# Differential attention of the last batch in pieces among the experts, and the order of the row chains' leads

## The chip, the cores and the metric

The kernel runs on one core of a Trainium2 chip, in fp32 throughout. The metric is device time in microseconds (us), the median of several runs. Engines: TensorE (PE; its weight loads are listed as PEld), VectorE (DVE), ScalarE (ACT), GpSimd (POOL) and SyncE (SP, which here only issues DMAs). A scatter or gather by index and an adding DMA are issued by POOL, all plain loads and stores by SP.

## The reference, cut to what matters

`x` has 8 batches of 512 positions of 128 numbers. There are two layers; in each, an attention and a feed-forward part read the same normalised `x`, and both are added to it. The change touches layer 1 alone.

```python
xn = layernorm(x)                            # layer 0 has been added to x
x  = x + diff_attn(xn) + ffn(xn)

def diff_attn(x):                            # for each batch, 512 x 512
    a = softmax(q1 @ k1.T * s) - lam * softmax(q2 @ k2.T * s)
    o = a @ v
    return o / sqrt(mean(o * o) + EPS) * 0.2

def ffn(h):                                  # "rows": along the 8 batches, for each position
    qkv = layernorm(h) @ Wqkv                # 16 query heads, 8 key/value heads
    h   = h + causal_attention(qkv) @ Wproj  # 8 x 8 scores for each position and head
    z   = layernorm(h)
    p   = softmax(z @ Wrouter)               # 8 experts, the best 2 of each token
    put z of each token into the slots of its two experts (1280 slots for each expert)
    for e in experts:                        # 128 -> 512 -> 128
        y = gelu(slots[e] @ W1[e]) @ W2[e] * weight
        add the rows of y to the rows of h they came from
    return h
```

The output is thus written in parts: `x` with the differential attention and `h` first, then the rows of the experts are added to it in DRAM.

## The kernel before, in words

**Stages on the trace.** Layer 0's feed-forward part and the projections run to about 278 us. A long loop over layer 0's attention follows to about 706; beside it run the first *row chains* of layer 1. A row chain is a generator for batch `s_` (its code begins above L690): normalise, project to `qkv`, eight products of the batch's query with all earlier keys on POOL (L722), each summed into a score buffer `sc` on DVE (L714 to L717), softmax, products with the values on POOL (L751) and their sums `l_at` on DVE (L760), a transpose `a1T_p` and a projection `pp` on TensorE (L782), the second normalisation, the router on POOL and TensorE (L812 to L889), and eight indirect DMAs (*puts*, L896) that write the batch's rows into the experts' slots `xs`. Chain 7 is the last. `sc` has one buffer, and L703 holds a chain until the chain before it has passed that point.

**Leads.** The chains in flight are `leads`. `step_leads` (L1162) is called once for each step of the main work and lets each lead do one piece, if the kind that it has named (`"pe"`, `"pool"`, `"dve"`, `"act"`) has room in this step; one POOL piece in all, given to the oldest lead that wants it.

**The tail** (L1374 to L1382) comes after the loop, from about 714 to 906 us. Its main work is the generator `diff(range(8))` (L1327): for each batch four projections `pqk` (L1246), a value `pv` (L1254), two scores `s` for each of four tiles of 128 queries (L1270) with a maximum on DVE (L1274) and an Exp on ACT (L1275), the combination of both on DVE (L1288), a transpose `dT`, an output `po` (L1304) and its squares on ACT (L1308). After the fourth tile POOL makes the reciprocal root `ri` (L1313 to L1316, four instructions), `diff_end` adds `po * ri` to `x_all` on DVE (L1321), and `store` sends the batch's 256 KB to the output by SP (L1369). The rows' chains 5, 6 and 7 are fed by `step_leads` at each step. The scores use the buffers "d" of PSUM, the projections and transposes the two buffers "t", the outputs "o".

`in_order(tail)` (L1382) then ties every instruction of the tail on PE, DVE, ACT and POOL to the one emitted before it on the same engine. So in the tail the order of emission is the order of execution. What is emitted after it, the experts, may be arranged by a scheduler.

**The experts** (L1391 to L1448), to the end: for each of eight experts a load `xe` of 1280 slots by SP (L1393, which waits for all puts), the slots' weights and row numbers on DVE (`first`, `wt`, `to`), and three blocks of 4, 4 and 2 tiles: a transpose with a copy `xeT` on DVE (L1413), up matmuls `phm` (L1421) with Gelu on ACT (L1424), down matmuls `pem` (L1428), a scaling `es` on DVE (L1434), and for each tile an indirect DMA on POOL (*scatter*, L1439) that adds 128 rows to the output. Scatters of one expert may overlap; those of the next one wait until all rows of the one before have landed, and expert 0's until all eight stores have.

```python
for name in backs[e] if e else bases:                                # L1446
    tc.add_manual_dep(back.ins, name, sync, ...)
```

Of the kernel before, what the change touches and what calls it, by code (L numbers as in the profile page):

```python
# [9 lines left out]
F32 = mybir.dt.float32  # L10
# [8 lines left out]
P = 128  # L19
# [6 lines left out]
def kernel(ctx: ExitStack, tc: tile.TileContext, a: dict, out: bass.AP):  # L26
# [579 lines left out]
    lw = {}  # L606
# [28 lines left out]
    def ln_stats(name, rows):  # L635
        stt = small.tile([P, 4, 6], F32, tag="bn_st", name=f"st_{name}")
        mv = small.tile([P, 4, 2], F32, tag="bn_mv", name=f"mv_{name}")
        for k, r in enumerate(rows):
            dve.bn_stats(out=stt[:, k, :], in_=r)
            dve.bn_aggr(out=mv[:, k, :], in_=stt[:, k, :])  # L640
            yield 1, "dve"
        yield 1, "pool"
        rs = small.tile([P, 4], F32, tag="bn_rs", name=f"rs_{name}")
        rsqrt(rs, mv[:, :, 1])
        nmr = small.tile([P, 4], F32, tag="nmr", name=f"nmr_{name}")
        nc.gpsimd.tensor_scalar(out=nmr, in0=mv[:, :, 0], scalar1=-1.0, scalar2=None, op0=ALU.mult)
        nc.gpsimd.tensor_tensor(out=nmr, in0=nmr, in1=rs, op=ALU.mult)
        yield 5, ""
        return mv, rs, nmr
# [15 lines left out]
    def lead(s_):  # L665
# [36 lines left out]
        yield 3, "pool"  # L702
        yield from after("sc", s_ - 1)  # L703
        sc = wt("sc", [NI * H, NB])
        q = qkv[:, s_, :, :, 0:2].rearrange("p i v r s -> p (i v) r s")
# [14 lines left out]
        for t in range(n):  # L720
            pr = prod("q", t)
            nc.gpsimd.tensor_tensor(out=pr, in0=of(t, 2), in1=q, op=ALU.mult)  # L722
            behind.append((t, pr))
            if len(behind) > BEHIND:
                yield 1, "dve"
                sum_q(*behind.pop(0))
            if t + 1 < n:
                yield 1, "pool"
# [20 lines left out]
        for t in range(n):  # L749
# [8 lines left out]
            if len(behind) > BEHIND:  # L758
                yield 1, "dve"
                dve.tensor_tensor(out=at4, in0=at4, in1=behind.pop(0), op=ALU.add)  # L760
# [129 lines left out]
        passed.add(("route", s_))  # L890
        yield 3, "pool"

        for i in range(NI):
            m = s_ * NI + i
            for k in range(2):
# [7 lines left out]
                puts.append(put.ins.name)  # L903
                yield 1, "pool"
        passed.add(("z2", s_))
# [3 lines left out]
    with ExitStack() as at:  # L909
# [251 lines left out]

        def step_leads(slot_, pe_free, pool_free, more):  # L1162
            room[0] = min(room[0] + more, more)
            spare[0] = min(spare[0] + more * SPARE, CAPA * more)
            for r in list(leads):
                if slot_ < r[1] or (r[2] == "pe" and not pe_free) or (r[2] == "pool" and not pool_free):
                    continue
                if r[2] == "dve" and room[0] <= 0 or r[2] == "act" and spare[0] <= 0:
                    continue
                if r[2] == "pool":  # L1170
                    pool_free = False
                nxt = next(r[0], None)
                if nxt is None:
                    leads.remove(r)
                else:
                    r[1], r[2] = slot_ + nxt[0], nxt[1]
# [49 lines left out]
    with ExitStack() as l1b:  # L1226
# [8 lines left out]
        cols = l1p["cols"]  # L1235
        wka = l1b.enter_context(tc.tile_pool(name="wka", bufs=2, reuse_waits="tile"))


        ascale = D ** (-0.25)
        OUT = (1.0 - LAMBDA_INIT) * math.sqrt(D)  # L1240
        dd = {}

        def diff_qk(b):
# [16 lines left out]
        def diff_scores(b, i):  # L1260
# [7 lines left out]
            for k in range(2):  # L1268
                sc = psum_t(f"s1_{u}_{k}", "d")
                nc.tensor.matmul(  # L1270
# [27 lines left out]
        def diff_out(b, i):  # L1298
            if i == 0:
                dd["po", b] = psum_o(f"po1_{b}")  # L1300
                dd["ss", b] = small.tile([P, NI], F32, tag="ss1", name=f"ss1_{b}")
            po, dT, ss = dd["po", b][:, i * D : (i + 1) * D], dd["dT", b, i], dd["ss", b]
            for c in range(NI):
                nc.tensor.matmul(  # L1304
                    po, lhsT=dT[:, c * P : (c + 1) * P], rhs=dd["v", b][:, c], start=(c == 0), stop=(c == NI - 1),
                )
            junk = wka.tile([P, D], F32, tag="sqj1", name=f"sqj1_{b}_{i}")
            nc.scalar.activation(junk, po, AF.Square, scale=1.0 / OUT, accum_out=ss[:, i : i + 1])  # L1308
# [9 lines left out]
        def diff_end(b):  # L1318
            po, ri = dd["po", b], dd["ri", b]
            for i in range(NI):  # L1320
                nc.vector.scalar_tensor_tensor(  # L1321
                    out=x_all[:, b, i], in0=po[:, i * D : (i + 1) * D], scalar=ri[:, i : i + 1],
                    in1=x_all[:, b, i], op0=ALU.mult, op1=ALU.add,
                )
            store(b)

        def diff(bs):  # L1327
# [8 lines left out]
            yield from diff_scores(*us[2])  # L1336
            more = diff_qk(bs[1])
            for m, (b, i) in enumerate(us):
# [29 lines left out]
        def store(b):  # L1368
            bases.append(  # L1369
                nc.sync.dma_start(out=out[b].rearrange("(i p) d -> p i d", p=P), in_=x_all[:, b]).ins.name  # L1370
            )

        slot_ = 4 * (N3 + 4)
        tail = len(nc.cur_bb.bb.instructions)  # L1374
        run = diff(range(NB))
        going = True
        while going or leads:
            going = next(run, "end") != "end"
            for _ in range(1):
                step_leads(slot_, True, True, 9.0)  # L1380
                slot_ += 1
        in_order(tail)  # L1382
        l1.close()
# [6 lines left out]
        backs = [[]]  # L1390
        for e in range(NE):  # L1391
            xe = wk.tile([P, NCT, W], F32, tag="xe", name=f"xe_{e}", bufs=3)
            get = nc.sync.dma_start(out=xe, in_=xs[e * CAP : (e + 1) * CAP].rearrange("(c p) d -> p c d", p=P))  # L1393
            for name in puts:
                tc.add_manual_dep(get.ins, name, sync, reason="any token may be in this expert's slots")

            first = small.tile([P, NCT], F32, tag="first", name=f"first_{e}", bufs=2)
            nc.vector.tensor_scalar(
# [6 lines left out]
            nc.vector.tensor_scalar(out=to, in0=xe[:, :, D + 2], scalar1=FAR, scalar2=None, op0=ALU.add)  # L1405
            es = wk.tile([P, NCT, D], F32, tag="es", name=f"es_{e}", bufs=4)
            backs.append([])
            for c0 in range(0, NCT, 4):
                n = min(4, NCT - c0)
                w = n * P  # L1410
                t = transpose4(f"xeT_p{e}_{c0}", [xe[:, c0 + k, :D] for k in range(n)])
                xeT = wk.tile([P, T], F32, tag="xeT", name=f"xeT_{e}_{c0}")
                nc.vector.tensor_scalar(  # L1413
                    out=xeT[:, :w], in0=t[:, :w], scalar1=cols[:, 2:3], scalar2=cols[:, 3:4], op0=ALU.mult, op1=ALU.add
                )
                hT = wk.tile([P, NHC, T], F32, tag="hTm", name=f"hTm_{e}_{c0}")
                for hp in range(NHC // 2):
                    ph = psum_s(f"phm_{e}_{c0}_{hp}")
                    for k in range(2):
                        hc = 2 * hp + k  # L1420
                        nc.tensor.matmul(  # L1421
                            ph[:, k, :w], lhsT=w1_1[:, e, hc * P : (hc + 1) * P], rhs=xeT[:, :w], start=True, stop=True
                        )
                    nc.scalar.activation(hT[:, 2 * hp : 2 * hp + 2, :w], ph[:, :, :w], AF.Gelu)  # L1424
                pe = psum_o(f"pem_{e}_{c0}")
                for k in range(n):
                    for hc in range(NHC):
                        nc.tensor.matmul(  # L1428
                            pe[:, k * D : (k + 1) * D], lhsT=hT[:, hc, k * P : (k + 1) * P], rhs=w2_1[:, e, hc, :],
                            start=(hc == 0), stop=(hc == NHC - 1),  # L1430
                        )
                for k in range(n):
                    c = c0 + k
                    nc.vector.tensor_scalar(  # L1434
                        out=es[:, c], in0=pe[:, k * D : (k + 1) * D], scalar1=wt_[:, c : c + 1], scalar2=None,
                        op0=ALU.mult,
                    )

                    back = nc.gpsimd.indirect_dma_start(  # L1439
                        out=out_rows, out_offset=bass.IndirectOffsetOnAxis(ap=to[:, c : c + 1], axis=0),  # L1440
                        in_=es[:, c], in_offset=None, bounds_check=NB * T - 1, oob_is_err=False,
                        compute_op=ALU.add,
                    )
                    tc.declare_no_dep(back.ins, group=f"backs{e}", reason="an expert's rows differ")
                    tc.add_to_no_dep_group(f"backs{e}", back.ins)
                    for name in backs[e] if e else bases:  # L1446
                        tc.add_manual_dep(back.ins, name, sync, reason="a row is read and written by each addition")
                    backs[e + 1].append(back.ins.name)  # L1448

# [36 lines left out]
```

## Time and profile before

| | us |
|---|---|
| median of the runs (3) | 1086.97 |
| lowest and highest run | 1086.4, 1087.47 |
| the profiled execution | 1084.87 |
| its span (first to last instruction) | 1083.1 |
| busy PE, PEld, DVE, ACT, POOL from 975 to 1035 us (one stretch of experts) | 58.4, 43.6, 15.2, 15.9, 45.2 of 60 |
| granted TensorE clock, mean of the span | 0.949 |

How to read it: the profile is one execution. A row of a timeline gives the start, the length, the engine, the line, the operation with output and input, and in brackets how long the engine had stood idle before it and what released it; "issue" means that nothing seen held it. "x8" is eight instructions in a row. An fp32 matmul shows as two records of TensorE, and the clock that the chip granted stands beside the work, as a share of full speed. The span ends with the landing of the last scatter. Landing times from issue, by the page's list: the slots' load 4.7 us, a store 2.2, a scatter 3.2, a put 2.3.

```profile
xe<-xs SPq DMA_DIRECT2D x8, 660.0 KB, 4.7
...
out_dram<-x_all SPq DMA_DIRECT2D x8, 256.0 KB, 2.2
out_dram<-es,to POOLq DMA_INDIRECT x80, 3.2
xs<-l_z,sput POOLq DMA_INDIRECT x64, 2.3
```

### The profile page before, as it was taken

The page shows a single profiled execution, that of the slowest core. Times are in us where ns is not written, and L with a number is a line of the kernel's source. Part 1 is how long each engine was busy: PE and PEld are TensorE (multiplying, and loading weights), DVE is VectorE, ACT ScalarE, POOL GpSimd, SP SyncE. Part 2 cuts the span into 40 slices and gives each one's busy share as a digit, 9 for nine tenths or more (in the row PEclk, how much of TensorE's full clock was granted, in tenths as well). Part 3 has the DMA queues.
Part 4 walks back from the last instruction along what each step waited for, and adds up shares of the span by engine and source line. Part 5 has one row for each costly group of instructions (what it writes and reads, how often), then busy time and mean ns, then how long its engine had stood idle before and what let it go on. Part 6 is the DMA issues. An engine that isn't in the chain of part 4 may idle for free.

```text
span 1083.1 us, 18816 instructions
## 1 busy us (share of the span) xinstructions
PE 974.5 (90%) x6726; PEld 599.0 (55%) x6726; DVE 664.2 (61%) x2126; ACT 553.0 (51%) x1263; POOL 565.6 (52%) x793
## 2 busy tenths in 40 slices
PE   6889899989999999999899999978867987999992
PEld 3457556867545454454444444435545655777772
DVE  6734643277777788888778887258676654222220
ACT  3466348353467576766565656527454653222220
POOL 3201000201242527775878879775867361777776
PEclk8999999999799999999999999779988998999997
DMA  8730000000000000000000000050000013342312
GB/s 252 158 85 2 1 1 1 2 2 1 1 1 2 2 1 2 21 2 2 14 9 3 19 2 21 2 172 1 20 11 20 21 38 103 49 67 38 31 15 25
DMA packets 49310, 32.97 MB, mean 30 GB/s; under 512 B 12232, under 2 KB 44275, under 8 KB 49216
## 3 DMA queue, kind: packets, MB, share of 16 engines
q1 hardware_dynamic: 34832, 24.80, 8.6%
q0 software_dynamic: 13568, 6.70, 4.5%
q8 instruction: 53, 0.87, 0.3%
q14 instruction: 41, 0.34, 0.1%
q10 hardware_dynamic: 816, 0.26, 0.1%
HBM read 17.56 MB, written 17.07 MB: 32 GB/s over the span
## 4 chain that ended last, share of the span: by engine, by line
PE 64%; POOL 14%; DVE 11%; issue 5%; ACT 2%; DMA 2%; POOLq 0%; DVEq 0%; SPq 0%; ACTq 0%
PE se L1068 12%; PE pem L1428 7%; PE phm L1421 6%; PE po L1093 6%; POOL xs L896 4%; PE sm L1035 3%; PE lg_d L302 3%; PE pe L477 3%; PE psl L346 3%; DVE junk L1045 2%; PE pf L379 2%; PE pq L955 2%; PE lg_c L302 2%; PE ph L451 2%; PE s L1270 2%
## 5 line engine op out<-in xcount | busy, mean ns | idle before, releaser
L1045 DVE CUSTOM_DVE_ANT_0 junk<-sm,cmask 128x128 f32<-128x128 f32 (+3 forms) x512 | 249.5, 487 | 69.3 <-PE sm L1035 31.2
L1073 ACT ACTIVATE pt<-se 128x384 f32<-128x384 f32 (+1 forms) x384 | 185.4, 527 | 158.7 <-PE sm L1035 109.7
L1035 PE MATMUL sm<-kj,qT 32*128 32x256 f32 (+3 forms) x1024 | 231.6, 487 | 5.7 <-DVE mcol L1045 3.0
L1068 PE MATMUL se<-q,kj 32*128 32x128 f32 (+3 forms) x1024 | 211.3, 483 | 3.9 <-DVE mcol L1045 3.5
L1439 POOL DMA_INDIRECT out_dram<-es,to x80 | 124.0, 1551 | 46.8 <-issue 22.8
L1068 PEld LDWEIGHTS se<-q,kj 32*128 32x128 f32 x1024 | 99.3, 190 | 84.7 <-DVE mcol L1045 26.1
L1078 POOL TENSOR_SCALAR_AFFINE_SELECT pt<-pt 128x512 f32<-128x512 f32 (+1 forms) x96 | 80.1, 835 | 115.8 <-ACT pt L1073 115.6
L1035 PEld LDWEIGHTS sm<-kj,qT 32*128 32x128 f32 x1024 | 112.6, 191 | 23.8 <-DVE mcol L1045 10.1
L1093 PE MATMUL po<-pt,vpad 128*18 128x512 f32 (+3 forms) x1024 | 91.4, 454 | 12.6 <-POOL pt L1078 12.6
L1424 ACT ACTIVATE hTm<-phm 128x1024 f32<-128x1024 f32 (+1 forms) x48 | 42.2, 881 | 109.2 <-PE phm L1421 109.2
L1428 PEld LDWEIGHTS pem<-w,hTm 128*128 128x128 f32 x640 | 77.1, 192 | 16.8 <-ACT hTm L1424 12.1
L1428 PE MATMUL pem<-w,hTm 128*128 128x128 f32 x640 | 81.2, 278 | 0.5 <-ACT hTm L1424 0.2
L1275 ACT ACTIVATE ex<-s,nm 128x512 f32<-128x512 f32 x64 | 43.9, 687 | 70.3 <-DVE nm L1274 69.7
L1434 DVE TENSOR_SCALAR es<-pem,wt 128x128 f32<-128x128 f32 x80 | 22.9, 345 | 90.0 <-PE pem L1428 90.0
L1421 PE MATMUL phm<-xeT,w 128*128 128x512 f32 (+1 forms) x192 | 75.2, 523 | 2.3 <-DVE xeT L1413 2.3
L896 POOL DMA_INDIRECT xs<-l_z,sput x64 | 65.8, 1028 | 17.0 <-issue 16.0
L508 POOL TENSOR_TENSOR x_all<-x_all,bo_bc 128x512 f32<-128x512 f32 x8 | 10.2, 1275 | 119.4 <-DVE xn L266 119.4
L1270 PE MATMUL s<-qk,qk 128*128 128x512 f32 x128 | 63.9, 620 | 6.6 <-ACT qk L1248 6.4
L1093 PEld LDWEIGHTS po<-pt,vpad 128*18 128x18 f32 x1024 | 20.9, 98 | 64.1 <-POOL pt L1078 24.0
L1274 DVE TENSOR_REDUCE nm<-s 128x1 f32<-128x512 f32 x64 | 42.9, 682 | 9.0 <-PE s L1270 8.6
L1421 PEld LDWEIGHTS phm<-xeT,w 128*128 128x128 f32 x192 | 33.6, 191 | 23.1 <-issue 17.2
L722 POOL TENSOR_TENSOR l_prod<-l_qkv 128x512 f32<-128x512 f32 x36 | 45.6, 1277 | 0.6 <-DVE l_at L616 0.6
(262 smaller groups left out, 1865.4 us busy)
## 6 DMA issues: line engine op xcount, KB each, us to landing
xs<-cmask SPq DMA_DIRECT2D x1, 5280.0 KB, 23.8
xe<-xs SPq DMA_DIRECT2D x8, 660.0 KB, 4.7
x_all<-in_L_attn_x_dram SPq DMA_DIRECT2D x8, 256.0 KB, 4.6
w<-in_L_ffn_w_dram SPq DMA_DIRECT2D x1, 2048.0 KB, 8.8
w<-in_L_ffn_moe_w_dram SPq DMA_DIRECT2D x1, 2048.0 KB, 10.0
out_dram<-x_all SPq DMA_DIRECT2D x8, 256.0 KB, 2.2
out_dram<-es,to POOLq DMA_INDIRECT x80, 3.2
xs<-l_z,sput POOLq DMA_INDIRECT x64, 2.3
```

What stands on the lines that cost most here:

```text
L302: nc.tensor.matmul(lg, lhsT=lhs(k), rhs=rhs, start=True, stop=True)
L896: put = nc.gpsimd.indirect_dma_start(out=xs, out_offset=bass.IndirectOffsetOnAxis(ap=sput[:, k, m : m + 1], axis=0), in_=z2[:, i], in_offs ...
L1035: nc.tensor.matmul(sc[:, o : o + w], lhsT=st["qT", b][rr, i * P : (i + 1) * P], rhs=st["k", b, j][rr, :w], start=True, stop=True,)
L1045: nc.vector.tensor_tensor_reduce(out=junk[:, :w], in0=sc[:, o : o + w], in1=cmask[:, 512 - w : 512], scale=-1.0, scalar=BIG, op0=ALU.add, ...
L1068: nc.tensor.matmul(sc[:, o : o + w], lhsT=st["k", b, j][rr, c * P : (c + 1) * P], rhs=st["q2", b, (g % G) // 2][rr, c * P : T], start=True ...
L1073: nc.scalar.activation(st["pt", g, k][:, r, :o], sc[:, :o], AF.Exp)
L1078: nc.gpsimd.affine_select(out=pt[:, :, :n, :P], in_=pt[:, :, :n, :P], pattern=[[0, 4], [0, n], [1, P]], compare_op=ALU.is_ge, fill=0.0, ba ...
L1093: nc.tensor.matmul(po[32 * r : 32 * r + 2 * PW, c * P : T], lhsT=vpads[b % 3][:, c, at_ : at_ + 2 * PW], rhs=pt[:, r, o : o + w], start=(c ...
L1270: nc.tensor.matmul(sc, lhsT=dd["qk", b, 2 * k][:, i * P : (i + 1) * P], rhs=dd["qk", b, 2 * k + 1], start=True, stop=True,)
L1421: nc.tensor.matmul(ph[:, k, :w], lhsT=w1_1[:, e, hc * P : (hc + 1) * P], rhs=xeT[:, :w], start=True, stop=True)
L1428: nc.tensor.matmul(pe[:, k * D : (k + 1) * D], lhsT=hT[:, hc, k * P : (k + 1) * P], rhs=w2_1[:, e, hc, :], start=(hc == 0), stop=(hc == NH ...
L1439: back = nc.gpsimd.indirect_dma_start(out=out_rows, out_offset=bass.IndirectOffsetOnAxis(ap=to[:, c : c + 1], axis=0), in_=es[:, c], in_of ...
```

## The change

1. **Row chains.** The score buffer `sc` is doubled, and a chain waits for the chain before the last. The kinds that a lead can name get three more: `"row"` and `"sum"` (as `"dve"` in the tail) and `"put"` (takes the POOL piece of a step). In the tail, leads that want a put come last in each step.
2. **Batch 7.** The tail runs `diff(range(7))`. Batch 7's differential attention is a second generator, `late`, stepped from the experts: two steps after the first half and one after the second half of a block's down matmuls, from the seventh of 24 blocks on. Its scores and outputs use the buffers "t"; its outputs are copied to SBUF by DVE. Its `diff_end` scales the copy in place, and `late_add` adds it to the output with one POOL DMA of 256 KB, after expert 6's scatters and before expert 7's. Its store of `x_all` is issued at the end of the tail, without the differential attention.
3. **Experts.** They are cut into functions and emitted as a pipeline: first half of the next block's up, first half of this block's down, second half of up, the transposes of the block after next, second half of down. The slots are loaded two experts ahead. `in_order(tail)` now comes after the experts, so that they too keep the order of emission.

```diff
         yield 3, "pool"
-        yield from after("sc", s_ - 1)
-        sc = wt("sc", [NI * H, NB])
+        yield from after("sc", s_ - 2)
+        sc = wt("sc", [NI * H, NB], bufs=2)
...
-        yield 3, "pool"
+        yield 3, "put"
...
-        def step_leads(slot_, pe_free, pool_free, more):
+        def step_leads(slot_, pe_free, pool_free, more, at_once=()):
...
-            for r in list(leads):
-                if slot_ < r[1] or (r[2] == "pe" and not pe_free) or (r[2] == "pool" and not pool_free):
+            for r in sorted(leads, key=lambda r: bool(at_once) and r[2] == "put"):
+                if slot_ < r[1] or (r[2] == "pe" and not pe_free) or (r[2] in ("pool", "put") and not pool_free):
                     continue
...
+        LATE = tuple(range(NB - 1, NB))
...
-                sc = psum_t(f"s1_{u}_{k}", "d")
+                sc = psum_t(f"s1_{u}_{k}", "d" if b not in LATE else "t")
...
+            to = dd["po", b][:, i * D : (i + 1) * D]
+            po = psum_t(f"po1_{b}_{i}")[:, :D] if b in LATE else to
...
+            if b in LATE:
+                nc.vector.tensor_copy(to, po)
...
             for i in range(NI):
+                if b in LATE:
+                    nc.vector.tensor_scalar(
+                        out=po[:, i * D : (i + 1) * D], in0=po[:, i * D : (i + 1) * D], scalar1=ri[:, i : i + 1],
+                        scalar2=None, op0=ALU.mult,
+                    )
+                    continue
...
-        run = diff(range(NB))
+        run = diff(range(LATE[0]))
...
-                step_leads(slot_, True, True, 9.0)
+                step_leads(slot_, True, True, 9.0, ('none',))
                 slot_ += 1
-        in_order(tail)
+        for b in LATE:
+            store(b)
...
+        def expert_up(e, c0, n, hp):
+            w, xeT = n * P, ee["xeT", e, c0]
+            if hp == 0:
+                ee["hT", e, c0] = wk.tile([P, NHC, T], F32, tag="hTm", name=f"hTm_{e}_{c0}")
+            ph = psum_s(f"phm_{e}_{c0}_{hp}")
...
+            nc.scalar.activation(ee["hT", e, c0][:, 2 * hp : 2 * hp + 2, :w], ph[:, :, :w], AF.Gelu)
...
+        late = diff(LATE)
+
+        def late_steps(n):
+            for _ in range(n):
+                next(late, None)
+
+        def late_add(e):
+
+            for _ in late:
+                pass
+            new = []
+            for b in LATE:
+                add = nc.gpsimd.dma_start(
+                    out=out[b].rearrange("(i p) d -> p i d", p=P),
+                    in_=dd["po", b].rearrange("p (i d) -> p i d", i=NI), accum_op=ALU.add,
+                )
+                for name in backs[e + 1]:
+                    tc.add_manual_dep(add.ins, name, sync, reason="a row is read and written by each addition")
+                new.append(add.ins.name)
+            backs[e + 1] = new
+
+        BLOCKS = [(e, c0, min(4, NCT - c0)) for e in range(NE) for c0 in range(0, NCT, 4)]
+        AFTER = 6
+        rows_get(0)
+        rows_get(1)
+        late_steps(0)
+        rows_in(0)
+        expert_T(*BLOCKS[0])
+        expert_T(*BLOCKS[1])
+        expert_up(*BLOCKS[0], 0)
+        expert_up(*BLOCKS[0], 1)
+        for m, (e, c0, n) in enumerate(BLOCKS):
+            if c0 == 0 and e + 2 < NE:
+                rows_get(e + 2)
+            half = range(n // 2), range(n // 2, n)
+            for hp in range(2):
+                if m + 1 < len(BLOCKS):
+                    expert_up(*BLOCKS[m + 1], hp)
+                if hp == 1 and m + 2 < len(BLOCKS):
+                    if BLOCKS[m + 2][1] == 0:
+                        rows_in(BLOCKS[m + 2][0])
+                    expert_T(*BLOCKS[m + 2])
+                expert_down(e, c0, n, half[hp])
+                late_steps(((2,1)[hp]) if m >= 6 else 0)
+            if e == AFTER and c0 + n == NCT:
+                late_add(e)
+        in_order(tail)
```

`rows_get`, `rows_in`, `expert_T` and `expert_down` hold the instructions of the old loop body: the load of the slots, their weights and row numbers on DVE, the transposes with their copy, and a half of the down matmuls, followed, once the block is whole, by its scalings and scatters.

## The prediction

> **What bounds the kernel now.** I read the page's slices first, then the windows of the last 370 us, then the timeline round each hole in TensorE. Rows of the page: engine totals, POOL in 40 slices of 27.1 us, two groups of indirect DMAs.
>
> ```profile
> PE 974.5 (90%) x6726; PEld 599.0 (55%) x6726; DVE 664.2 (61%) x2126; ACT 553.0 (51%) x1263; POOL 565.6 (52%) x793
> POOL 3201000201242527775878879775867361777776
> L1439 POOL DMA_INDIRECT out_dram<-es,to x80 | 124.0, 1551 | 46.8 <-issue 22.8
> L896 POOL DMA_INDIRECT xs<-l_z,sput x64 | 65.8, 1028 | 17.0 <-issue 16.0
> ```
>
> TensorE at 90% suggests that only its work matters. The windows (start:end, length, then busy PE, PEld, DVE, ACT, POOL, then granted clock) say otherwise for the end:
>
> ```profile
> 820.00:840.00 20.00, 13.98 (x60) 8.80 (x59) 10.68 (x20) 10.12 (x30) 13.10 (x16) 0.90 0.04 13
> 840.00:860.00 20.00, 20.00 (x95) 12.84 (x94) 13.46 (x34) 14.20 (x40) 5.92 (x10) 0.93 0.05 14
> 975.00:1035.00 60.00, 58.39 (x343) 43.56 (x342) 15.21 (x49) 15.86 (x18) 45.22 (x31) 1.00 0.29 34
> 1064.00:1083.00 19.00, 0.41 (x4) 0.22 (x2) 0.61 (x2) 0.00 (x0) 12.62 (x9) 0.61 0.35 31
> ```
>
> From 706 to 838 TensorE has holes, from 838 to 889 none, and in the last 19 us only POOL works. The holes are the row chains' (columns: start, length, engine, line, operation, idle before and its releaser):
>
> ```profile
> 790.35 2.08 PE L1270 MATMUL s<-qk,qk 128*128 128x512 f32 x2 [6.37 <-ACT qk L1248]
> ...
> 812.47 1.92 PE L1246 MATMUL pqk<-xn,wk 128*128 128x512 f32 x2
> ...
> 830.65 0.97 POOL L896 DMA_INDIRECT xs<-l_z,sput  x1 [0.31 <-issue]
> ...
> 837.51 1.09 PE L141 MATMUL a1T_p<-ident,l_at 128*128 128x128 f32 x4 [6.02 <-DVE l_at L616]
> ```
>
> The transpose at 837.51 belongs to row chain 7 and stands in TensorE's queue ahead of half of the diff attention. It waits for POOL products that sit behind eight puts (821.58 to 831.63). After it 68.8 us of TensorE work follow, to 906.3.
>
> At the end, scatters:
>
> ```profile
> 1057.17 1.55 POOL L1439 DMA_INDIRECT out_dram<-es,to  x1 [0.30 <-issue]
> 1060.84 1.55 POOL L1439 DMA_INDIRECT out_dram<-es,to  x1 [2.12 <-DMA out_dram<-es,to]
> ...
> 1077.51 1.55 POOL L1439 DMA_INDIRECT out_dram<-es,to  x1 [0.30 <-issue]
> ```
>
> One scatter each 1.85 us, 3.67 where a new expert must see the last one's rows land: 9 x 1.853 + 3.67 = 20.35 us per expert. TensorE's first up matmul of every second expert stands at 935.08, 974.49, 1013.90 and 1053.32: 19.7 us per expert. So POOL binds this stage, by a hair. Experts start on TensorE at S = 908.1, the first scatter at S + 10, the last at 1077.5, the end 5.6 later: S + 175.
>
> **Sum, part 1: the tail with seven batches.** Up to the first matmul of the tail every engine's order is the same, so all before about 706 stands. Ahead of chain 7's last product POOL loses batch 6's puts (8 x 1.28 = 10.2), batch 6's routing (about 10.6 by its rows from 800.3 to 819.5) and one reciprocal root group with its neighbours (2.7): 23.5 us, so 837.5 becomes 814. The second score buffer lets chain 7's first products run in the gaps of chain 6; before, DVE stood waiting for them 5.9 us and TensorE for what follows 6.4. I take 10 for it: **804**. Bounds: 781 (TensorE's 58.5 us of work from 722, no hole) and 815 (the buffer gives nothing).
>
> Queued on TensorE behind that transpose, by the changed order: 28 score matmuls at 0.86, 12 projections at 0.86, 3 values and 19 outputs at 0.89, 17 transposes at 0.44, 2 for the rows: 63.5. With the transpose 0.4, a stretch at half clock 2.8 and the drain of the last batch 2.5 this gives **873** (867 to 882), against 906.3. So 33 us earlier: 16.5 because batch 7 (8 scores, 4 projections, 1 value, 4 transposes, 4 outputs) is gone from here, 17 from the rows. The puts of batch 7, now last, need some 10 us of POOL and 2.3 to land; the rows for expert 0 (4.7 to landing) are still there about 15 us before 873. On SP five stores now precede the first three expert loads, each 2.2 us and done by then: nothing.
>
> Before, expert 0's transposes ran on TensorE before batch 7's last output. Held in order, DVE does the last diff_end (1.1, after the root on POOL 1.75 and a square 0.5), then the rows' weights (0.5), then the transposed copy (0.8): 4.7 us with no TensorE work. **S = 878.**
>
> **Part 2: batch 7 among the experts.** Pure work of an expert is 40 down products x 2 x 0.113 + 8.6 of up + 1.1 of transposes = 18.8; with the 3% that today's 19.7 loses only in part, 19.3. Let X be the end of expert 4's first down block: 4 experts and 11.6 us of the fifth, 89. By then 14.8 of batch 7's 16.5 us are in. POOL, 20.35 per expert, would need S + 99 for the same point; TensorE comes there later, so the pieces are not hidden: scatters run out of rows.
>
> Stalls in it: the pieces bring Exp between the Gelus, ten more table loads. The trace's row is 1.28 us, starting only when the matmul for it is done (the load at 910.06 had waited 3.33 for it) and with the Gelu directly behind. The Trainium skill, "ScalarE: Activation LUTs", sections "What ACT_TABLE_LOAD costs" and its list of advice, speaks against the change: group by table set, and budget a drain of 1.38 with each load, 2.66 in all. By the row 12.8, by the page 26.6. No drain stands behind the load in this trace, so I take the row. While ACT loads, the two buffers of the scores and transposes stay occupied; with two up buffers as cover for about half, 6.4 is exposed (0 to 12.8; by the page 13, thus 7 more). The hole at S costs half clock, as at 812.47, where two projections took 1.92 instead of 1.02 after a hole: +1.7 at both such places. X = S + 89 + 14.8 + 6.4 + 1.7 = **S + 112 = 990**.
>
> Then a new wait. The root for batch 7 (four POOL instructions) is placed behind four scatters of expert 4, which come free at X: 4 x 1.85 + 1.75 + starting 0.6 = X + 9.8. On DVE the scaling of batch 7 (4 instructions, 1.1) waits for it, and behind it in DVE's order stand expert 5's weights and its first transposed copy, and expert 4's next results. TensorE has 7.5 us of work left, then waits until X + 12.3: 4.9 us, and 1.7 of half clock. Six scatters of expert 4 start at X + 13.5, expert 5's first at X + 27.
>
> From there POOL binds: experts 5 and 6 take 2 x 20.35, expert 7's nine pitches 16.7, the last landing 5.6, and between 6 and 7 the accumulating add of 256 KB. No such DMA is in the trace. "DMA: Bandwidth & Descriptors", "Anatomy of one DMA — SWDGE (gpsimd) path", gives 2.0 + bytes/436e3 = 2.6 (estimate from the page); the nearest rows are four scatters' worth of rows plus a landing, 4 x 1.55 + 2.1 = 8.3, and the plain 256 KB store, 2.2 to landing, plus the wait of 2.1: 4.3. It needs no index per row, so I take the store's, with the handover, 6: by the page 4, by the scatters 10. End = X + 27 + 40.7 + 6 + 16.7 + 5.6 = **X + 96 = 1086**. The stage takes S + 208 instead of S + 175: it gives back the 33.
>
> Span 1086.4; the profiled execution lies 1.8 outside its span (1084.87 against 1083.1), and the median of the runs is 2.1 above that execution: **1090**. Own range 1081 to 1101: stalls 0 to 12.8 (6.4 either way), the tail -6 to +9, the add -2 to +4, not all at once.
>
> **Rivals.** *Faster* (F), two ways to one end. The rows may come free at TensorE's pace (781): the tail ends near 855 and all follows 18 earlier, 1072. Or batch 7 slips under the scatters: if POOL bound throughout, S + 12.5 + 146.4 + 7 turns of 1.8 + 6 + 5.6 = S + 184 = 1062, median 1066. That is decided by how far TensorE is ahead of POOL at expert 2's start: it needs about 20 us; 19.7 against 20.35 gives 1.3. For the first speaks that POOL loses a fifth of its work there; against it, DVE and POOL disturb each other (the row chains' additions take 1.11 us on the mean in this stretch, 0.69 in the median of all).
>
> *Much slower* (R): the rows do not come free. DVE stays the limit, chain 7 ends at 815 or later, the tail at 885, and all is 12 later: 1102. For it: the products of both chains meet on one POOL, and one step in the order still holds one POOL piece. It decides if chain 7's transpose stands after 812.
>
> *The change does nothing in the main loop* (N): the second buffer and the late puts could have moved things before 706; the instruction order shows they don't, so no gain or loss there.
>
> **From cases to numbers.** Likeliest case, 1081 to 1101, 0.55; F 0.25; R 0.2. A difference of 0.2%, 2.2 us, is about what can be told from none. The likeliest case is centred 3 us above before: of its 0.55 some 0.1 is faster, 0.15 the same, 0.3 slower. With F faster and R slower: 0.33, 0.15, 0.52. The range takes in most of F's first way and R: 1074 to 1103.
>
> **What would show it.** Right: chain 7's transpose near 804, TensorE free of the tail near 873, a hole of about 5 us before the first up matmul; in the experts POOL idle between scatters from the third expert on, one hole of 5 us on TensorE after expert 4's first block released by DVE, the last TensorE work 13 us or more before the end. Wrong: POOL at one scatter per 1.85 us all through (F), TensorE holes of more than 3 us at each Exp (stalls mis-sized), or the transpose after 812 (R).

## The result

| | before | after |
|---|---|---|
| median of 8 runs, us | 1087.19 | 1094.17 |
| ratio of the times | | 1.0068, 95% interval 1.0057 to 1.0078 |
| the profiled execution, us | 1084.87 | 1093.88 |
| its span, us | 1083.1 | 1092.2 |

The changed kernel is 0.7% slower. The forecast was 1090, slower, between 1074 and 1103. Direction and size came out; two of its terms were wrong, in opposite directions, so that the nearness of the number is in part luck.

The page of the kernel after, two of the rows that were shown of before (the scatter's source line has moved from L1439 to L1472):

```profile
PE 980.6 (90%) x6726; PEld 603.6 (55%) x6726; DVE 668.4 (61%) x2130; ACT 568.3 (52%) x1273; POOL 567.4 (52%) x794
L1472 POOL DMA_INDIRECT out_dram<-es,to x80 | 124.4, 1555 | 69.7 <-DVE es L1467 40.6
```

POOL does the same work, but it now stands 69.7 us before its scatters where it stood 46.8, and for most of that it waits for a row to scatter (`es`), not for its own queue. A window of the kernel after (as before: start:end, length, busy PE, PEld, DVE, ACT, POOL, granted clock):

```profile
975.00:1035.00 60.00, 54.94 (x330) 41.88 (x329) 19.99 (x61) 19.44 (x32) 39.85 (x29) 0.97 0.22 27
```

From 975 to 1035 POOL is busy 39.9 of 60 us instead of 45.2. The TensorE rows with the holes:

```profile
809.95 0.90 PE L141 MATMUL a1T_p<-ident,l_at 128*128 128x128 f32 x4 [2.55 <-DVE cc L1286]
846.09 0.41 PE L864 MATMUL prank<-seen,ones 128*128 128x32 f32 x2 [2.06 <-POOL seen L857]
...
891.07 7.24 PE L1444 MATMUL phm<-xeT,w 128*128 128x512 f32 x12 [2.73 <-DVE xeT L1433]
...
1008.30 3.57 PE L1444 MATMUL phm<-xeT,w 128*128 128x512 f32 x4 [4.86 <-DVE xeT L1433]
```

Chain 7's transpose stands at 810 instead of 837.5, the first up matmul at 891.1 instead of 908.1: the experts start 17 us earlier. The end is 201.1 us behind that matmul instead of 175.0: the experts take 26 us more.

**Where the 26 us are.** The first scatter of each expert stands at 904.5, 927.7, 949.0, 972.6, 996.6, 1024.0, 1044.4 and 1069.6. Against the 20.35 us of an expert whose scatters follow without a gap, the distances exceed by 2.9, 1.0, 3.2, 3.6, 7.1, 0 and 4.9, together 22.7. The first scatter itself stands 13.4 us behind the first up matmul instead of 10.0. That is 26.1. The two large ones, on POOL:

```profile
1002.13 1.54 POOL L1472 DMA_INDIRECT out_dram<-es,to  x1 [0.31 <-issue]
...
1004.62 1.04 POOL L129 TENSOR_TENSOR ri<-ri,powers 128x4 f32<-128x4 f32 x1
1008.70 1.65 POOL L1472 DMA_INDIRECT out_dram<-es,to  x1 [3.04 <-DVE es L1467]
...
1060.99 1.54 POOL L1472 DMA_INDIRECT out_dram<-es,to  x1 [0.30 <-issue]
1064.48 1.38 POOL L1495 DMA_DIRECT2D out_dram<-po  x1 [1.95 <-DMA out_dram<-es,to]
1069.64 1.64 POOL L1472 DMA_INDIRECT out_dram<-es,to  x1 [3.79 <-DVE es L1467]
```

The root of batch 7 comes behind the fourth scatter of expert 4, and the fifth then lacks its row; DVE shows why. Its scaling of batch 7 waits 5.0 us for the root, and expert 5's transposed copy and expert 4's next rows (`es`) queue behind it:

```profile
1005.69 0.87 DVE L1328 TENSOR_SCALAR po<-po,ri 128x128 f32<-128x128 f32 x4 [5.01 <-POOL ri L129]
...
1007.35 0.81 DVE L1433 TENSOR_SCALAR xeT<-xeT_p,cols 128x512 f32<-128x512 f32 x1
1008.07 1.12 DVE L1467 TENSOR_SCALAR es<-pem,wt 128x128 f32<-128x128 f32 x4
```

The adding DMA is issued at 1064.48 and expert 7's first scatter at 1069.64, where 3.68 us lie between two experts without it.

### The profile page after: what moved, and what is told of

It is laid out like the page before. It is cut to its first block, busy times and chain, and to the rows that moved or that the text cites. A ratio compares the mean times of both kernels' runs of the same rounds, so it can differ in the third digit from the quotient of the medians.

```text
span 1092.2 us, 18828 instructions
## 1 busy us (share of the span) xinstructions
PE 980.6 (90%) x6726; PEld 603.6 (55%) x6726; DVE 668.4 (61%) x2130; ACT 568.3 (52%) x1273; POOL 567.4 (52%) x794
## 5 line engine op out<-in xcount | busy, mean ns | idle before, releaser
L1472 POOL DMA_INDIRECT out_dram<-es,to x80 | 124.4, 1555 | 69.7 <-DVE es L1467 40.6
L1444 PE MATMUL phm<-xeT,w 128*128 128x512 f32 (+1 forms) x192 | 80.3, 544 | 8.1 <-DVE xeT L1433 7.6
L1459 PE MATMUL pem<-w,hTm 128*128 128x128 f32 x640 | 78.9, 275 | 0.0
L1433 DVE TENSOR_SCALAR xeT<-xeT_p,cols 128x512 f32<-128x512 f32 (+1 forms) x24 | 17.2, 720 | 80.0 <-PE xeT_p L141 80.0
```

Of the source, the lines that this page charges most:

```text
L1444: nc.tensor.matmul(ph[:, k, :w], lhsT=w1_1[:, e, hc * P : (hc + 1) * P], rhs=xeT[:, :w], start=True, stop=True)
L1459: nc.tensor.matmul(pe[:, k * D : (k + 1) * D], lhsT=hT[:, hc, k * P : (k + 1) * P], rhs=w2_1[:, e, hc, :], start=(hc == 0), stop=(hc == NH ...
L1472: back = nc.gpsimd.indirect_dma_start(out=out_rows, out_offset=bass.IndirectOffsetOnAxis(ap=ee["to", e][:, c : c + 1], axis=0), in_=es[:, ...
```

## The experiments

The kernel before, run again beside each group of runs that follows, had medians of 1085 to 1091 us, so ratios to it are compared. Within profiles there is another spread. Take as t0 the start of the row chain's projection `pqkv` (L690) that stands some 19 us ahead of the tail's first `pqk`. Up to it all kernels issue the same instructions in the same order, yet it starts anywhere from 692.5 to 700.7 us. The table therefore counts from t0, in us; "by t0" below means a difference of its column "end".

| kernel | t0 | tail's last output | first up matmul | first scatter | end | ratio to before (95%) |
|---|---|---|---|---|---|---|
| before | 694.9 | 211.3 | 213.2 | 223.2 | 388.2 | 1 |
| after | 696.4 | 190.3 | 194.7 | 208.1 | 395.9 | 1.0068 (1.0057 to 1.0078) |
| late_off | 696.1 | 206.0 | 210.4 | 224.9 | 391.6 | 1.0016 (0.9999 to 1.0033) |
| rows_only | 695.9 | 212.9 | 214.7 | 224.7 | 389.9 | 1.0025 (1.0009 to 1.0040) |
| rows_undone | 699.8 | 189.6 | 206.7 | 220.2 | 407.7 | 1.0169 (1.0130 to 1.0209) |
| end_later | 697.8 | 189.4 | 193.9 | 206.5 | 389.1 | 1.0017 (1.0000 to 1.0034) |
| no_add | 696.2 | 189.1 | 193.5 | 207.9 | 390.4 | 1.0005 (0.9974 to 1.0036) |
| pieces_last | 700.6 | 189.1 | 193.5 | 207.9 | 383.0 | 0.9940 (0.9917 to 0.9963) |
| pieces_18 | 696.6 | 189.1 | 193.5 | 207.9 | 383.1 | 0.9934 (0.9905 to 0.9963) |
| pieces_14 | 700.7 | 189.2 | 193.6 | 208.0 | 381.8 | 0.9943 (0.9919 to 0.9967) |
| fill_start | 695.1 | 190.2 | 200.8 | 213.3 | 388.8 | 0.9997 (0.9978 to 1.0016) |
| puts_old | 694.0 | 189.9 | 194.3 | 207.6 | 395.0 | 1.0076 (1.0059 to 1.0093) |
| one_buffer | 695.0 | 180.7 | 185.1 | 199.4 | 388.1 | 0.9941 (0.9924 to 0.9957) |
| best | 692.5 | 177.6 | 182.0 | 196.2 | 370.8 | 0.9828 (0.9805 to 0.9852) |

**1. Are the pieces a gain at all? late_off** keeps the rows' change and the held experts, but does batch 7 in the tail.

```diff
-        LATE = tuple(range(NB - 1, NB))
+        LATE = ()
...
-            if e == AFTER and c0 + n == NCT:
-                late_add(e)
```

> Changed kernel with batch 7's differential attention back in the tail and no adding DMA; rows, held experts and look-ahead stay. Mine (the pieces cost more among the experts than they save in the tail): TensorE leaves the tail 16.5 us later than in the changed kernel, the scatters then run at about 20.4 to 21 us per expert from the third expert on, and the excess of expert 5's turn (7.1 us) and of the add (5.0) are gone; time about 1090 to 1092, 2 to 4 below the changed kernel. Rival (holding the experts in order is what loses, the pieces are harmless): first scatters of two experts stay 23 us and more apart all through, time 1094 to 1110, at or above the changed kernel.

It came as expected: 4.3 us below the changed kernel by t0, five thousandths by ratio; the scatters run at 20.2 to 21.0 us per expert from the second distance on. Moving batch 7 shortens the tail by 15.7 us and lengthens the experts by 20: a net loss where it is put. The other 6 of the experts' 26 us late_off has too (181.2 us from the first up matmul to the end, 175.0 before): they come with the new order of the experts, not with batch 7.

**2. The rows' change alone. rows_only** is the kernel before with the second score buffer and the puts last. **rows_undone** is the changed kernel without them.

```diff
-        yield from after("sc", s_ - 2)
-        sc = wt("sc", [NI * H, NB], bufs=2)
+        yield from after("sc", s_ - 1)
+        sc = wt("sc", [NI * H, NB])
...
-                step_leads(slot_, True, True, 9.0, ('none',))
+                step_leads(slot_, True, True, 9.0)
```

> Kernel before with the second score buffer and the puts last, nothing else. Mine (the rows come free some 25 us earlier, but most of that turns into half clock and smaller holes in TensorE's tail): chain 7's transpose at 808 to 812, TensorE leaves the tail 2 to 5 us earlier than before, time 1082 to 1085. Rival (the rows were the tail's limit, so what they gain the tail gains): 10 us or more, 1070 to 1077. Second rival (late puts hold up the load of expert 0's slots): 1087 or more.

> Changed kernel with one score buffer and puts in their old place among the leads. Mine: chain 7's transpose back near 836, 12 to 16 us of TensorE work is left behind it in the tail less than before, so the tail ends 2 to 6 us later than in the changed kernel: 1096 to 1100. Rival (the rows' change is worth the whole 17 us that the forecast gave it): 1105 to 1112.

Both expectations missed. rows_undone landed where its rival had put it, but not for the rival's reason. Together they say what the rows' change does. In rows_only chain 7's transpose is 29 us earlier (113.7 after t0 instead of 142.6), and the tail is no shorter. In rows_undone the tail is as long as in the changed kernel, and still the kernel takes 12 us more. TensorE of rows_undone, then its last put on POOL:

```profile
904.49 1.94 PE L141 MATMUL xeT_p<-ident,xe 128*128 128x128 f32 x8 [15.03 <-DMA xe<-xs]
```

```profile
897.01 0.97 POOL L896 DMA_INDIRECT xs<-l_z,sput  x1 [0.30 <-issue]
```

With batch 7 gone, TensorE leaves the tail at 889 and the last put is issued at 897: expert 0's slots are loaded too late. The rows' change brings the last put to 859.5. It opens the load; it does not shorten TensorE's tail.

The kernel before and rows_only have a hole that is not the rows' either. Its experts are not held, so their first DVE instruction, which waits for the slots' load, may be placed among the tail's. DVE and TensorE of rows_only:

```profile
866.67 0.17 DVE L1400 TENSOR_SCALAR first<-xe 128x10 f32<-128x10 f32 x1 [8.31 <-DMA xe<-xs]
```

```profile
870.14 2.07 PE L1272 MATMUL s<-qk,qk 128*128 128x512 f32 x2 [5.73 <-ACT qk L1250]
```

Between them stands ACT, whose Exp waits for the maximum and whose copy `qk` for TensorE comes behind that Exp; then the like hole of the kernel before:

```profile
867.90 0.69 ACT L1277 ACTIVATE ex<-s,nm 128x512 f32<-128x512 f32 x1 [5.00 <-DVE nm L1276]
...
869.49 0.60 ACT L1250 ACTIVATE qk<-pqk 128x512 f32<-128x512 f32 x1
```

```profile
896.40 1.09 PE L141 MATMUL dT_p<-ident,ex 128*128 128x128 f32 x4 [6.93 <-DVE wt L1403]
```

The maxima of the tail's scores queue behind `first`, and TensorE stands 5.7 us, in the kernel before 6.9. late_off, whose experts are cut up and held in order, has no such hole: 206.0 against 212.9. In exchange its first scatter stands 14.5 us behind the first up matmul and the next expert's 22.0 behind that, against 10.0 and 20.4. No run separates the hold from the new order of emission.

**3. The two parts of it apart. puts_old** keeps the second buffer alone (only the second part of the diff above), **one_buffer** keeps the puts last alone (only the first part).

> Changed kernel with the puts in their old place among the leads, the second score buffer kept. Mine (the two parts only matter by when the last put of batch 7 lands, as the load of expert 0's slots waits for it; each part gives about half of the 15 us hole seen without both): TensorE's tail as long as in the changed kernel, a hole of 0 to 8 us before expert 0's transposes, 1094 to 1102. Rival (one of the two carries it all): no hole and the changed kernel's time, or the 15 us hole and 1106 to 1110.

> Changed kernel with one score buffer, puts last kept. Mine: as the run with the puts in their old place, a hole of 5 to 12 us before expert 0's transposes, 1098 to 1106. Rival: no hole and the changed kernel's time, or the 15 us hole.

Neither part acts as I thought. The buffer alone (puts_old) gives the changed kernel's time, as its rival had it: it carries all of the load's gain. The puts last alone (one_buffer) do too, with the last put at 866.7, and end the tail 9.6 us earlier, which neither its expectation nor its rival had: this one edit puts the changed kernel 0.6% below before. So the second buffer costs 9 us or more where the puts are last, and nothing where they are not (189.9 with two buffers, 189.6 with one in rows_undone). The profile of one_buffer is of the slowest of its five runs, 6 us above their median: by ratio it lies 1.3% below the changed kernel, by t0 only 7.8 us. Windows of the changed kernel, two of 10 us and one from t0 to its last output, and the same of one_buffer (columns as above):

```profile
795.00:805.00 10.00, 8.23 (x34) 5.93 (x35) 5.68 (x15) 3.16 (x9) 9.29 (x11) 0.66 0.03 10
805.00:815.00 10.00, 7.42 (x31) 4.79 (x30) 6.77 (x17) 6.16 (x18) 7.57 (x20) 0.83 0.09 27
...
696.35:886.63 190.28, 158.48 (x735) 101.55 (x735) 128.46 (x277) 98.78 (x275) 131.29 (x202) 0.90 0.17 50
```

```profile
795.00:805.00 10.00, 8.85 (x43) 5.09 (x43) 8.71 (x18) 5.64 (x17) 9.48 (x15) 1.00 0.09 27
805.00:815.00 10.00, 5.99 (x13) 3.45 (x14) 7.91 (x15) 3.54 (x11) 9.03 (x18) 0.67 0.01 2
...
694.97:875.64 180.67, 151.39 (x736) 95.74 (x736) 127.17 (x277) 98.09 (x275) 132.57 (x202) 0.93 0.17 48
```

With two buffers TensorE has several small holes (2.3 and 1.8 us at 795 and 797, 2.6 at 810, 2.1 at 846) and the granted clock falls behind each cluster. With one it has a hole of 4.1 at 809 and then runs unbroken to 870. From t0 to the last output the holes sum up to 31.5 against 29.0 us. The work is the same instructions, yet TensorE is busy 158.5 us against 151.4: the other 7.1 of the 9.6 us is the same work at a lower clock, 0.90 against 0.93 on the mean. best, with the same tail as one_buffer, has 149.6 us at 0.93. That the buffer does this is shown by undoing it, in two kernels (tails of 180.7 and 177.6 us, against 189.1 to 190.3 in the seven with two buffers and the puts last); why the two chains' products, interleaved, leave these holes just there was only argued from the order of the queues.

**4. The root's wait. end_later** holds the scaling of batch 7 back to just before the add.

```diff
-            for _ in range(n):
+            for _ in range(min(n, left[0])):
                 next(late, None)
+                left[0] -= 1
...
         late = diff(LATE)
+        left = [22]
```

> Changed kernel with the four scalings of batch 7 (and only them) held back to just before the adding DMA, so that DVE goes on to expert 5's weights and transposed copy without waiting for the root behind four scatters. Mine (that wait is worth the 7.1 us by which expert 5's first scatter is late): 1086 to 1088, and the hole of 4.9 us before expert 5's first up matmul is gone. Rival (POOL is the limit there, TensorE's hole is hidden): 1093 to 1095.

The distance from expert 4 to 5 falls from 27.45 to 22.19, and the hole of 4.9 us is gone. By t0 it is 6.8 us, of which 1.6 lie already ahead of the first scatter. The wait in DVE's queue was the cause of 5.3 of the 7.1 us; the root on POOL stayed where it was, and the 1.8 us left over 20.35 are about what its four instructions take there.

**5. The add. no_add** leaves the adding DMA out, and with it batch 7's differential attention in the output.

```diff
-            new = []
...
-            backs[e + 1] = new
```

> Changed kernel without the adding DMA: batch 7's differential attention is computed but left out of the output. Mine (the add lengthens the turn from expert 6 to 7 by 5.0 us and all scatters behind it): 1088 to 1090, 4.5 to 5.5 below the changed kernel. Rival (the wait for expert 6's rows is the larger part and stays, the DMA itself is hidden): within 2 us of the changed kernel.

As expected: 5.5 us by t0, and the distance from expert 6 to 7 falls from 25.28 to 20.46; the ratio's interval is wide, but it lies below the changed kernel's.

**6. The place of the pieces. pieces_last, pieces_18 and pieces_14** put the add behind expert 7 and the pieces behind the last block, from block 18, and from block 14 with one step for each half.

```diff
-        AFTER = 6
+        AFTER = 7
...
-                late_steps(((2,1)[hp]) if m >= 6 else 0)
+                late_steps(1 if m >= 14 else 0)
```

> Changed kernel with all pieces of batch 7 emitted after the last block of expert 7, and the adding DMA after expert 7's scatters. Mine (POOL binds the experts as soon as TensorE has no extra work, and TensorE is done some 20 us before the last scatter, so the pieces lie under the scatters there): scatters 20.4 us per expert from expert 1 or 2 on, last scatter near 904.5 + 162 = 1066, the root, the scaling, the add and its landing 8 to 10 after it: span 1074 to 1078, 8 to 12 below before. Rival (the pieces' Exp between Gelus or the serial chain of one batch alone is what costs, wherever they stand): TensorE needs 30 us or more for them after the last block, span 1085 or more.

> The same, but the pieces begin at block 18 of 24 (expert 6) in the changed kernel's rhythm, add after expert 7. Mine: TensorE is ahead of the scatters by some 15 us when expert 6 begins, so no scatter starves until expert 7's last blocks, and batch 7 is ready before the last scatter: span 1072 to 1077, at or a little below the kernel with all pieces last. Rival (table loads between Exp and Gelu stall TensorE): 5 us or more above it.

> The same, from block 14 on, one step for each half of a block. Mine: TensorE's lead over the scatters is about 1 us per expert plus the first expert's, so at expert 5 it is near 8 to 10 us; the pieces eat it slowly and the scatters starve little: span 1073 to 1080. Rival (any piece among the experts delays a scatter): 1083 or more.

All three are 13 to 14 us below the changed kernel and, within their intervals, equal; the diff is that of pieces_14. The same pieces that cost scatters at block 6 cost next to none at the end, since TensorE is done 22 us before the last scatter there (1060.1 and 1082.1 in late_off). The gain against before is 6 us, less than the 8 to 12 expected. In pieces_last the last scatter starts 370.0 us after t0, and 1066 would be 369.6; but from there to the end it is 13.1 us (11.6 and 11.7 in the other two), not the 8 to 10 expected for root, scaling, add and landing. The held start (first scatter 14.4 us behind the first up matmul, the next expert 23.2 behind that) costs too, but was in that sum, which began at the measured 904.5.

**7. The start. fill_start** is pieces_14 with the first five pieces emitted between expert 0's transposes and its first up matmul.

```diff
...
-        late_steps(0)
         rows_in(0)
         expert_T(*BLOCKS[0])
         expert_T(*BLOCKS[1])
+        late_steps(5)
```

> The kernel with pieces from block 14 and the add after expert 7, with one more edit: the four projections and the value of batch 7 are emitted between expert 0's first transposes and its first up matmul. Mine (at the start TensorE stands 3.6 us and then runs at half clock; 4.3 us of its work fit there and keep the clock): first scatter 2 to 3 us earlier after the tail's end, 2 to 4 us less than the kernel with pieces from block 14, ratio to before about 0.991. Rival (the start is held by DVE and the first Gelu's table load, not by TensorE): no change, ratio 0.994.

Missed: 7 us slower than pieces_14. TensorE of fill_start:

```profile
885.18 1.04 PE L141 MATMUL xeT_p<-ident,xe 128*128 128x128 f32 x8
889.78 1.12 PE L1248 MATMUL pqk<-xn,wq 128*128 128x512 f32 x2 [3.56 <-DVE xeT L1433]
```

The projections use the same two buffers "t" that the transposes hold until DVE has copied them. So they can't run in the hole; they come behind it and push the up matmul back.

**8. Both findings together. best** is pieces_14 with one score buffer.

> One score buffer with the puts last, batch 7's pieces from block 14 on with one step for each half of a block, and the adding DMA after expert 7. Mine (the two findings are in different stages and add up: the tail ends 9 us earlier than with two buffers because TensorE keeps its full clock there, and the late pieces lie under the scatters): from the first projection of the tail to the end 373 us, ratio to before 0.984 to 0.987. Rival (an earlier tail only makes the scatters the longer pole, or the slots' load is late again): ratio 0.990 to 0.995.

1065.13 us median (1064.66 to 1069.79), the best of all: 1.7% below before. From t0 to the end it is 370.8 us, a little less than the 373 expected, and the two gains add up: by their ratios one_buffer and pieces_14 lie 1.27% and 1.25% below the changed kernel, best 2.40%. The tail is 12.7 us shorter than the changed kernel's, and its scatters follow at 20.2 to 20.9 us per expert after the first. POOL at its end:

```profile
1051.69 1.55 POOL L1472 DMA_INDIRECT out_dram<-es,to  x1 [0.30 <-issue]
...
1054.18 1.04 POOL L129 TENSOR_TENSOR ri<-ri,powers 128x4 f32<-128x4 f32 x1
1056.43 1.40 POOL L1495 DMA_DIRECT2D out_dram<-po  x1 [1.21 <-DVE po L1328]
```

The root now waits for the last scatters to be issued, and the add ends the kernel 11.6 us after the last scatter's start, instead of the 5.6 of the kernel before.

## Why the prediction was right, and where not

- **The sum.** The first up matmul came 13 us later than forecast (891.1 instead of 878), and the stretch from it to X 7 us shorter (105 instead of 112), so that X and the end came 6 us late (1092.2 instead of 1086.4). The median lay 0.3 us above the profiled execution instead of 2.1, which took about 2 of the 6 back. Two slips of the sum did not matter: F's second way adds up to S + 183, and the chances to 0.35, 0.15 and 0.50.
- **What binds.** Right: from expert 5 on POOL's scatters bind, and before, while the pieces last, scatters run out of rows (first scatters 23.6 and 24.0 us apart from expert 2 to 4).
- **The tail, part 1.** The term "17 from the rows" failed. Chain 7's transpose came near its forecast (113.6 us after t0; 804 would be 109.1), but from there to the last output it took 77 us instead of 69, with holes of 5.0 us and three stretches at half clock, and an earlier transpose did not shorten the tail: with the rows undone it is as long. What the tail gained is 15.7 from batch 7 (16.5 forecast) and 5.3 that late_off gains on before, where the hole of the slots' load is gone. That hole (6.93 us, 889.5 to 896.4) lies in the 68.8 us that the forecast took for TensorE work behind the transpose. The last output came at 886.6 instead of 873, 1.4 of it from a later t0. The forecast held the load of the slots for hidden with 15 us to spare, which is true only thanks to the earlier puts: a gain that I gave to the wrong resource.
- **The start of the experts.** 4.7 us without work were forecast; from the last output to the first up matmul it is 4.4, but only 2.7 of it without work, since expert 0's transposes stand there.
- **The stalls of the table loads.** The term of 6.4 was too large, and offset half of the first miss. From the first up matmul to the end of expert 4's first block (X, 995.9) TensorE waited 1.7 us in all. ACT and TensorE of the kernel after:

```profile
955.74 1.28 ACT L1447 ACT_TABLE_LOAD   x1
957.03 1.02 ACT L1447 ACTIVATE hTm<-phm 128x1024 f32<-128x1024 f32 x1
```

```profile
960.20 0.66 PE L141 MATMUL xeT_p<-ident,xe 128*128 128x128 f32 x4 [1.49 <-ACT ex L1277]
```

  Ten loads of 1.28 us, and only one keeps TensorE waiting over 1 us. The Gelu starts 0.01 us behind the load: there is no drain of 1.38 us, so the row was to be taken and not the 2.66 us of the Trainium skill ("ScalarE: Activation LUTs", "What ACT_TABLE_LOAD costs"), whose advice to group by table set ("Rules for kernel authors") weighed little here. One of the ten loads (973.97) was over 1.4 us before its Exp's input came, so a load does not always start only when its input is ready, as the forecast had it.
- **The root's wait.** Right in place and size: hole of 4.9 us forecast, 4.86 measured; expert 5's first scatter at X + 27, measured X + 28.
- **The add.** 6 us forecast, 5.0 measured, 5.5 by leaving it out. The estimate of 2.6 us from the Trainium skill ("DMA: Bandwidth & Descriptors", "Anatomy of one DMA — SWDGE (gpsimd) path"), 4 with the handover, would have been low, four scatters' worth, 10, high. To landing it took 4.4 us, twice the store's 2.2:

```profile
out_dram<-po POOLq DMA_DIRECT2D x1, 256.0 KB, 4.4
```

- **From X to the end.** 96 forecast, 96 measured.
- **The rivals.** F's second way names the price at which it decides, a TensorE lead of 20 us over POOL at expert 2's start. There it is about 5: expert 2's first scatter starts 5.6 us behind the last down matmul of its first block, where a scatter that waits for nothing else starts 0.7 behind it. A lead of 20 us exists only at the end of the experts (22 us in late_off); pieces_last to pieces_14 put the work late enough to use what lead there is. R did not happen as told: the transpose came before 812. Its tail end of 885 did come (886.6), for other reasons, and its 1102 did not.

## What to carry to other kernels

Work that is moved under a bound engine is free only where the engine that does it is ahead: here TensorE gains 1 to 2 us per expert on POOL after the first. In late_off the third expert's first scatter starts 5.1 us behind the last down matmul of its block, the eighth's 12.4, and the last scatter of all 22.0. When work leaves a stage, look at what else the next stage waits for; the rows' change paid through a DMA's input and not through the engine whose hole it closed. In a queue held in order, an instruction with a slow input (a root behind scatters, a value behind a load) makes all behind it wait, so it belongs as late as its reader allows.

## What the hardware showed that was not expected

The same holes were followed by half clock in one execution and by full clock in another. one_buffer and best issue the same tail in the same order. A window of one_buffer, then of best:

```profile
785.00:795.00 10.00, 5.58 (x32) 3.54 (x31) 7.19 (x13) 4.33 (x12) 8.35 (x11) 1.00 0.06 17
```

```profile
785.00:795.00 10.00, 7.69 (x34) 5.49 (x33) 7.18 (x18) 6.00 (x18) 8.62 (x12) 0.66 0.14 40
```

In one_buffer the window has holes of 2.05 and 2.36 us, which end at 788.4 and 792.3; in best the same two are 2.07 and 2.31 us long and end at 784.3 and 788.1. The score that follows the second takes 1.13 us in one_buffer and 2.07 in best. And a hole of 3.43 us at 740 in the changed kernel leaves full clock (1.00 from 735 to 755), where those of 2.3 and 1.8 us at 795 and 797 leave 0.66. So the cost of a hole cannot be read from its length in these traces; what decides it is open. And t0 moved between executions by up to 8 us under one and the same instruction order, which is more than most of the effects studied here.
